# Attention weights of a four-layer graph network: the broadcast exponential moved from the scores to the weights, and due times taken from a backward play of the plan

## The chip, the cores and the metric

The kernel runs on one core of one Trainium2 chip, as one launch. A core has a matrix engine (TensorE, PE in the profile), a vector engine (VectorE, DVE), an engine for activation functions (ScalarE, ACT), a general one (GpSimd, POOL) and a queue engine that only issues transfers (SyncE, SP). Each works through its own instructions in the order in which the program gives them, and waits for the others by semaphores. The metric is the time of one execution on the device in microseconds (us).

## The reference

There are 64 graphs of 256 nodes with 256 features each (x, float32) and their adjacency matrices (adj, int32, about one entry in 64 is 1, the rest 0). Four layers follow each other, and each is added to x:

```python
h = relu(layernorm(x));  x = x + GAT0(h, adj)     # 4 heads of 64, slope 0.2, elu
h = relu(layernorm(x));  x = x + GAT1(h, adj)     # 4 heads of 64, slope 0.01, relu + residual, layer norm per head
h = relu(layernorm(x));  x = x + GAT2(h, adj)     # 1 head of 256, slope 0.2
h = relu(layernorm(x));  x = x + GRU(h, adj)      # 3 steps: aggregate adj^T (h w_i), then a GRU cell
```

An attention layer projects h to Wh, takes two scores of each node, `s` (as source) and `d` (as target), and weighs the neighbours by a softmax:

```python
e = leaky_relu(s[:, None] + d[None, :], slope)
alpha = softmax(where(adj > 0, e, -1e9), axis=-1)
out = alpha @ Wh
```

A GRU cell has six gate products of 256 by 256 per step: three from the aggregate and three from the state.

## The kernel before

**Tiling.** The 64 graphs are split into 33 units: one graph, 31 pairs of graphs, one graph. A unit goes through all four layers, and several units are in work at a time, so that one unit's matrix work fills the other's waits. Nodes lie on the 128 partitions; a pair has C = 4 chunks of 128 nodes.

**The weights.** exp(leaky_relu(s + d)) isn't computed as written. With a = slope, exp(max(t, a t)) for t = s + d is the larger of exp(s) exp(d) and exp(a s) exp(a d); a factor that depends only on the node whose softmax it is cancels, so that one needs only max(f0, f1 · cb): `f0` = exp(score) and `f1` = exp(a · score) of the node on the partition, and `cb` = exp((a − 1) · score of the target), the same on all partitions. The adjacency enters as a `cap`: where there is no edge the cap is tiny, and the minimum of weight and cap masks it.

`factors` makes these. The scores are columns of the projected tile `wh`. For the first SPREAD = 2 units TensorE spreads the target's scores over all partitions into a PSUM bank (`spread`, matmuls L1092), and ScalarE writes the exponential of it to `cb` (L1099). For the others TensorE transposes the score columns (L1111), ScalarE takes the exponential of the short `row` (L1118), a DMA on ScalarE's queue stores it to DRAM (`rd`, L1123), and a DMA on SP's queue loads it back to all partitions (L1124; 1024 KB for a pair with 4 heads, 256 KB with one). Two small ScalarE exponentials make f0 and f1 (L1130).

`weights` makes one head's tile `pt`. For each graph and each chunk of 128 nodes there is one VectorE TENSOR_SCALAR over 128 x 256 elements, cb times f1, then max with f0 (L1145); then one TENSOR_TENSOR over the whole head of a pair (128 x 1024) takes the minimum with `cap`. `attend` multiplies pt with wh (L1163).

**The order.** Nothing is issued as it is written. Every operation is recorded in `_Schedule` with its engine, a cost in ns and the buffers that it reads and writes; then `run` plays the program forward on modelled engines. At each free engine it takes the operation with the earliest due time that is ready and whose buffers have a free slot, and the resulting order is what each engine gets. Results are visible to another engine after OVERLAP + HOP (370, 240, 240 and 270 ns for PE, ACT, DVE and POOL); a DMA takes 2000 ns plus its bytes at 220 per ns. Due times come from one pass backwards over the operations: the due time of a follower less STRETCH (3.13) times its cost less MARGIN (800), counted from the end of the unit, which is set by PACE (104000 ns per pair). Operations with `port=True` (VectorE's and GpSimd's with shared access) aren't planned at the same time.

**Names in the profile.** `vec` records most VectorE and GpSimd operations and `op` some of ScalarE's, so many instructions carry L829. The layer norm is L997 (statistics on VectorE), L1006 and L1007 (GpSimd), L1015 (ScalarE, out `xn` or, ahead of the GRU, `hn`), its transposition L1032. The projection is L1054 (PE, with weights `w0e`, `w1e`, `w2e` by layer) and the copies L1067 and L1069. In the first 75 us PE also multiplies weight matrices (L949) and a few columns (L927). Layer 0 loads xt and the adjacency `at`, makes `am` (L1220), `cap_n` (L1214, L1230) and its transposition. Layer 1's norm per head is L1296 and L1297 (GpSimd, tile `mean`). The GRU splits the state in two parts (`hl`, L1346, `split`), aggregates (L1361, copied to `ag`), and multiplies the gates (L1375, in `bank`, with `ht` the transposed state); ScalarE's activations make `g` from `bank` and VectorE combines them; L1389 transposes states and outputs (`rows_of`), L1449 stores the output. Pools have a few slots: 8 PSUM banks, 5 `xt`, 4 `pt`, 2 `cb` for 4 heads.

Of the kernel before, what the change touches and what calls it, by code (L numbers as in the profile page):

```python
# [518 lines left out]
SPREAD = 2  # L519
PACE = 104000.0  # L520
# [8 lines left out]
class _Buf:  # L529


    def __init__(self, cls, shape, dtype, tile=None):
        self.cls, self.shape, self.dtype, self.tile = cls, shape, dtype, tile
        self.parts = {}
        self.left = 0
        self.slot = None


class _Op:
    __slots__ = (  # L540
        "engine", "cost", "port", "emit", "group", "bufs", "takes", "nbytes", "succs", "waits", "due", "ready",
        "index",
# [3 lines left out]
class _Schedule:  # L546
# [10 lines left out]

    OVERLAP = {"pe": 0, "act": 90, "dve": 80, "pool": 0, "sp": 0}
    HOP = {"pe": 370, "act": 240, "dve": 240, "pool": 270, "sp": 0}
# [3 lines left out]
    STRETCH = 3.13  # L563
    MARGIN = 800.0

    def __init__(self, tc, pools):

        self.tc, self.pools = tc, pools
        self.last = {}
        self.free = {cls: list(range(n)) for cls, (_, n) in pools.items()}  # L570
        self.ops = []
        self.group = 0
        self.end = {}
# [4 lines left out]
    def op(self, engine, cost, emit, reads=(), writes=(), takes=(), nbytes=0, port=False):  # L578
        o = _Op()
        o.port = port  # L580
        o.engine, o.cost, o.emit, o.group, o.nbytes = engine, cost, emit, self.group, nbytes
        o.succs, o.index, o.ready = [], len(self.ops), 0.0
        deps, o.bufs, o.takes = set(), [], []
        for written, items in ((False, reads), (True, writes)):
            for item in items:
                b, part = item if isinstance(item, tuple) else (item, None)
                if b not in o.bufs:
                    o.bufs.append(b)
                    b.left += 1
                if written and b.tile is None and b not in o.takes:  # L590
                    o.takes.append(b)
                keys = list(b.parts) if part is None else [k for k in (part, None) if k in b.parts]
                for k in keys:
                    writer, readers = b.parts[k]
                    if writer is not None:
                        deps.add(writer)
                    if written:
                        deps.update(readers)
# [7 lines left out]
        for b in takes:  # L606
            if b.tile is None and b not in o.takes:
                o.takes.append(b)
        deps.discard(o.index)
        o.waits = len(deps)  # L610
        for d in deps:
            self.ops[d].succs.append(o)
# [22 lines left out]
    def enable(self, ops, able):  # L635
        for o in ops:
            o.waits -= 1
            if o.waits == 0:
                heapq.heappush(able[o.engine], (o.due, o.index))

    def roomy(self, o):
        need = {}
        for b in o.takes:
            if b.tile is None:
                need[b.cls] = need.get(b.cls, 0) + 1
        return all(len(self.free[c]) >= n for c, n in need.items())

    def start(self, o, clock):
        for b in o.takes:
            if b.tile is None:  # L650
                b.slot = heapq.heappop(self.free[b.cls])
                b.tile = self.pools[b.cls][0].tile(b.shape, b.dtype, name=f"{b.cls}{b.slot}")
        self.issue(o)
        self.trace.append((clock, o))

    def run(self):
        ops = self.ops
        for o in reversed(ops):
            late = self.end[o.group]
            for s in o.succs:  # L660
                if s.group == o.group or o.group not in self.end or o.group < 0:
                    late = min(late, s.due - self.STRETCH * s.cost - self.MARGIN)
            if o.nbytes:
                late -= self.DMA_LATENCY + o.nbytes / self.DMA_RATE
            o.due = late
        engines = ("pe", "act", "dve", "pool", "sp")
        able = {e: [] for e in engines}
        idle = dict.fromkeys(engines, True)
        events = []
        clock = self.dma_free = self.port_free = 0.0  # L670
        count = 0
# [5 lines left out]

        for o in ops:
            if o.waits == 0:
                heapq.heappush(able[o.engine], (o.due, o.index))  # L680
        done = 0
        self.trace = []
        while True:
            for e in engines:
                if not idle[e]:
# [848 lines left out]
```

## Time and profile before

| what | us |
|---|---|
| three runs | 3197.56, 3197.72, 3199.27 (median 3197.72) |
| the profiled execution | 3199.95 |
| its span, first to last instruction | 3198.1 |
| GpSimd busy in the span | 897.4 |
| gate matmuls (L1375), share of the chain that ended last | 55% |
| granted TensorE clock, mean | 0.996 |

The span is what the trace covers; the execution's time has 1.85 us around it. The chain that ended last is found by going back from the last instruction, at each step to what released it:

```profile
PE 87%; DVE 9%; POOL 2%; ACT 1%; issue 1%; DMA 0%; SPq 0%; ACTq 0%; POOLq 0%; DVEq 0%
```

In 40 equal slices of 80 us, each digit the busy share in tenths, TensorE, VectorE and ScalarE look like this:

```profile
PE   7899999999999999999999999999999999999998
DVE  7777867778767778767678677788677787677753
ACT  5454444454454444454444454544444444544433
```

A row of the views by line gives the line, the engine, the operation, out<-in by the program's names, the shapes, the count, the busy time in us and the mean duration of one in ns, then the idle time of the engine just before these instructions and what ended it. In the timeline a row gives the start, the length, the engine, the line and the count, and in brackets the idle time before.

### The profile page before, as it was taken

Reading aid. Unit: us, or ns where it says so; the run is one execution under the profiler, and the core shown is the slowest. Engines: PE = TensorE matmul, PEld = TensorE weight load, DVE = VectorE, ACT = ScalarE, POOL = GpSimd, SP = SyncE. Lnnn points to the kernel's source line nnn. Section 1 sums busy time; section 2 is a strip of 40 time slices with the busy share of each in tenths; the row PEclk is TensorE's granted clock in tenths of the full one; section 3 lists DMA queues with packets and bytes.
Section 4 is the critical chain, followed back from the end, with each engine's and each line's share of the span. In section 5 each row is a group of like instructions: output and inputs, shape, how many; then the busy total and the mean of one; then the engine's idle time right before and its main releaser. Section 6 shows DMA issues by size and latency. Waiting matters only on the chain.

```text
span 3198.1 us, 48707 instructions
## 1 busy us (share of the span) xinstructions
PE 3143.2 (98%) x18599; PEld 1931.9 (60%) x18599; DVE 2321.4 (73%) x5206; ACT 1486.8 (46%) x3128; POOL 897.4 (28%) x907
## 2 busy tenths in 40 slices
PE   7899999999999999999999999999999999999998
PEld 6765656565666655566656566556566556665555
DVE  7777867778767778767678677788677787677753
ACT  5454444454454444454444454544444444544433
POOL 4323332133331233331233321333311333311210
PEclk9999999999999999999999999999999999999999
DMA  4110111101111101111101111111111011101000
GB/s 129 34 49 29 54 54 34 47 31 50 54 54 34 47 31 50 54 47 34 53 28 54 53 36 45 40 41 54 54 34 47 31 50 50 47 23 44 11 16 12
DMA packets 109927, 138.82 MB, mean 43 GB/s; under 512 B 44714, under 2 KB 97524, under 8 KB 102004
## 3 DMA queue, kind: packets, MB, share of 16 engines
q1 hardware_dynamic: 105712, 134.25, 12.8%
q8 instruction: 149, 2.44, 0.3%
q10 hardware_dynamic: 3972, 1.36, 0.2%
q14 instruction: 94, 0.77, 0.1%
HBM read 109.84 MB, written 17.34 MB: 40 GB/s over the span
## 4 chain that ended last, share of the span: by engine, by line
PE 87%; DVE 9%; POOL 2%; ACT 1%; issue 1%; DMA 0%; SPq 0%; ACTq 0%; POOLq 0%; DVEq 0%
PE bank L1375 55%; PE bank L1054 10%; PE bank L1163 10%; PE bank L1361 5%; PE bank L1032 3%; PE bank L1389 2%; DVE pt L1145 2%; DVE g L829 2%; DVE pt L829 1%; POOL mean L1297 1%; POOL o L829 1%; DVE o L829 1%; ACT ht L829 1%; DVE xt L1308 1%; DVE mean L829 1%
## 5 line engine op out<-in xcount | busy, mean ns | idle before, releaser
L1375 PE MATMUL bank<-ag,wc 128*128 128x512 f32 (+1 forms) x2376 | 1063.0, 582 | 0.0
L1375 PE MATMUL bank<-ht,whh 128*128 128x512 f32 (+1 forms) x2376 | 1055.6, 580 | 2.2 <-ACT g L829 1.3
L829 ACT ACTIVATE g<-bank,bg 128x512 f32<-128x512 f32 (+1 forms) x594 | 395.2, 670 | 713.6 <-PE bank L1375 706.6
L1375 PEld LDWEIGHTS bank<-ag,wc 128*128 128x128 f32 x2376 | 441.4, 190 | 459.2 <-issue 441.1
L1375 PEld LDWEIGHTS bank<-ht,whh 128*128 128x128 f32 x2376 | 435.0, 190 | 438.9 <-issue 424.2
L1006 POOL TENSOR_SCALAR mv<-mv 128x4 f32<-128x4 f32 (+1 forms) x132 | 81.9, 621 | 1428.6 <-DVE mv L998 1383.6
L1145 DVE TENSOR_SCALAR pt<-cb,f 128x256 f32<-128x256 f32 x1152 | 416.9, 430 | 6.0 <-ACT cb L1099 5.2
L1163 PEld LDWEIGHTS bank<-wh,pt 128*64 128x64 f32 (+1 forms) x8704 | 345.6, 142 | 94.4 <-issue 76.1
L829 DVE SCALAR_TENSOR_TENSOR g<-g,g 128x512 f32<-128x512 f32 (+1 forms) x396 | 263.3, 670 | 180.4 <-ACT g L829 180.4
L1163 PE MATMUL bank<-wh,pt 128*64 128x65 f32 (+1 forms) x8704 | 382.0, 233 | 9.7 <-DVE pt L829 5.8
L829 DVE TENSOR_TENSOR pt<-pt,cap 128x1024 f32<-128x1024 f32 (+1 forms) x297 | 341.3, 1193 | 0.1
L829 DVE SCALAR_TENSOR_TENSOR g<-bank,g 128x512 f32<-128x512 f32 (+1 forms) x198 | 129.8, 666 | 280.2 <-PE bank L1375 280.0
L829 DVE SCALAR_TENSOR_TENSOR g<-g,ht 128x512 f32<-128x512 f32 (+1 forms) x198 | 136.5, 689 | 172.0 <-ACT g L829 171.6
L1361 PE MATMUL bank<-am_r,hl 128*128 128x256 f32 x1536 | 238.1, 304 | 0.1
L1015 ACT ACTIVATE xn<-xt,mv 128x256 f32<-128x256 f32 x384 | 197.3, 588 | 72.1 <-DVE mv L829 71.9
L1361 PEld LDWEIGHTS bank<-am_r,hl 128*128 128x128 f32 x1536 | 198.2, 189 | 42.5 <-issue 30.6
L829 ACT COPY ag<-bank 128x512 f32<-128x512 f32 (+1 forms) x198 | 113.4, 573 | 233.4 <-PE bank L1361 230.1
L829 ACT ACTIVATE g<-g,bg 128x512 f32<-128x512 f32 (+1 forms) x198 | 137.6, 709 | 161.6 <-DVE g L829 159.4
L997 DVE BATCH_NORM_STATS2 st<-xt 128x6 f32<-128x256 f32 x512 | 208.1, 406 | 6.4 <-DMA xt<-in_x_dram 6.2
L829 ACT COPY ht<-bank 128x512 f32<-128x512 f32 (+1 forms) x264 | 137.8, 573 | 124.0 <-PE bank L1032 123.8
L1136 POOL MEMSET wh<- 128x16 f32 (+3 forms) x99 | 11.8, 120 | 635.5 <-ACT f L1130 635.5
L1007 POOL TENSOR_TENSOR mv<-mv,nhalf 128x4 f32<-128x4 f32 (+1 forms) x132 | 176.0, 1333 | 11.0
(91 smaller groups left out, 3452.2 us busy)
## 6 DMA issues: line engine op xcount, KB each, us to landing
cb<-rd SPq DMA_DIRECT2D x60, 1024.0 KB
xt<-in_x_dram SPq DMA_DIRECT2D x31, 512.0 KB
at<-in_adj_dram SPq DMA_DIRECT2D x31, 512.0 KB
out_dram<-xt SPq DMA_DIRECT2D x31, 512.0 KB
cb<-rd SPq DMA_DIRECT2D x30, 256.0 KB
cap<-cap_n SPq DMA_TRANSPOSE x128
cb<-rd SPq DMA_DIRECT2D x2, 512.0 KB
rd<-row ACTq DMA_DIRECT2D x60, 8.0 KB
```

What stands on the lines that cost most here:

```text
L829: emit = lambda: fn(*[a() if callable(a) else a for a in args], **kw)
L997: nc.vector.bn_stats(st.tile[:, c, :], xt.tile[:, c, :])
L1006: nc.gpsimd.tensor_scalar(mv.tile[:, 2, :], mv.tile[:, 1, :], 1e-5, None, op0=OP.add)
L1007: nc.gpsimd.tensor_tensor(mv.tile[:, 2, :], mv.tile[:, 2, :], nhalf[:, :C], op=OP.pow)
L1015: op("act", 610, lambda: nc.scalar.activation(xn.tile[:, c, :], xt.tile[:, c, :], AF.Relu, bias=mv.tile[:, 3, c : c + 1], scale=mv.tile[:, ...
L1032: nc.tensor.transpose(ps.tile[:, c * P : (c + 1) * P], xn.tile[:, c, dc * P : (dc + 1) * P], ident)
L1054: nc.tensor.matmul(ps.tile[:, : heads * W], lhsT=ht.tile[:, dc, c * P : (c + 1) * P], rhs=we[:, dc].rearrange("p h w -> p (h w)"), start=( ...
L1145: nc.vector.tensor_scalar(pt.tile[:, b, jc, :].rearrange("p (i n) -> p i n", n=P), cb.tile[:, h, 2 * b : 2 * b + 2, :], f.tile[:, 1, h, c ...
L1163: nc.tensor.matmul(ps[q * Q : (q + 1) * Q], lhsT=pt.tile[:, b, jc, i0 : i0 + Q], rhs=wh.tile[:, h, 2 * b + jc, :w], start=(jc == 0), stop= ...
L1361: nc.tensor.matmul(ps.tile[:, b * N : (b + 1) * N], lhsT=hl.tile[:, k, 2 * b + sc, :], rhs=am.tile[:, 2 * b + sc, :], start=(k == 0 and sc ...
L1375: nc.tensor.matmul(ps.tile[:, :S], lhsT=w[:, dc, g * P : (g + 1) * P], rhs=v.tile[:, dc, :], start=(first and dc == 0), stop=(last and dc ...
L1389: nc.tensor.transpose(ps.tile[:, c * P : (c + 1) * P], ht.tile[:, j, c * P : (c + 1) * P], ident)
```

## The change

It has three parts.

1. **The weights.** The target's score is broadcast as it is, without an exponential. ScalarE then computes exp((a − 1) · target's score + a column) for every graph, chunk and head (128 x 256), where the column is now the logarithm of the old f1, a · score plus a constant. One VectorE operation in place (SCALAR_TENSOR_TENSOR, 128 x 256) takes the max with f0 and the min with cap; the multiply-and-max and the wide minimum are gone. f1's small exponential becomes a small VectorE operation, the exponential of the row a copy.
2. **The first units.** SPREAD goes from 2 to 3. Units below it have no `cb`: ScalarE reads the scores of each head from the PSUM bank, which is held until all its weights are made.
3. **The planner.** `play` is the old forward play, without issuing anything. `latest` plays the program backwards from its end, taking operations by their start times of the last play, latest first, and gives each its latest start; these are the next play's due times. `run` makes up to 7 plays and issues the order of the one with the shortest modelled span. HOP becomes 310, 180, 180 and 210, PACE 100000, STRETCH 3.46. The part of `split` in the diff calls the same operations as before.

Counted over the program, VectorE loses 1152 TENSOR_SCALAR of 128 x 256, 279 TENSOR_TENSOR of 128 x 1024 and 18 of 128 x 512, and gets 1152 SCALAR_TENSOR_TENSOR of 128 x 256 and 99 small operations. ScalarE gets 1152 exponentials of 128 x 256, 90 of them from PSUM, and loses 18 copies of `cb` and 99 small exponentials. Three stores `rd` and three loads `cb` go; TensorE has 72 more matmuls in `spread` and 3 transposes fewer.

```diff
-SPREAD = 2
-PACE = 104000.0
+SPREAD = 3
+PACE = 100000.0
...
-    HOP = {"pe": 370, "act": 240, "dve": 240, "pool": 270, "sp": 0}
+    HOP = {"pe": 310, "act": 180, "dve": 180, "pool": 210, "sp": 0}
...
-    STRETCH = 3.13
+    STRETCH = 3.46
     MARGIN = 800.0
+    ROUNDS = 7
...
+    def lag(self, o, s):
+        if o.nbytes:
+            return self.DMA_LATENCY + o.nbytes / self.DMA_RATE
+        return 0 if o.engine == s.engine == "pe" else self.OVERLAP[o.engine] + self.HOP[o.engine]
...
+    def latest(self, starts):
+        left = {o.index: len(o.succs) for o in self.ops}
+        able = {e: [] for e in self.ENGINES}
...
+        def ready(o):
+            heapq.heappush(able[o.engine], (-starts[o.index], o.index))
...
+                o = self.ops[index]
+                if pred >= 0:
+                    left[pred] -= 1
+                    if left[pred] == 0:
+                        ready(self.ops[pred])
+                    continue
+                idle[o.engine] = True
+                for p in sorted(o.preds):
+                    heapq.heappush(events, (clock + self.lag(self.ops[p], o), count, p, index))
+        span = max(before_end.values())
+        return {i: span - t for i, t in before_end.items()}
...
+    def run(self):
+        due = self.paths()
+        self.span = float("inf")
+        for _ in range(self.ROUNDS):
+            trace, slots, span = self.play(due)
+            if span < self.span:
+                self.trace, taken, self.span = trace, slots, span
+            elif span == float("inf"):
+                break
+            due = self.latest({o.index: clock for clock, o in trace})
...
-                op("pe", pe(880), emit, [wh], [ps], takes=[cb])
-                op("act", act(700), lambda: nc.scalar.activation(
-                    cb.tile[:, h].rearrange("p c n -> p (c n)"), ps.tile[:, :S], AF.Exp,
-                    scale=slope - 1.0, bias=-shift * (slope - 1.0),
-                ), [ps], [(cb, h)])
+                op("pe", pe(880), emit, [wh], [ps])
+                return ps

             if u < SPREAD:
-                for h in range(heads):
-                    spread(h)
+                cb = [spread(h) for h in range(heads)]
...
-                    nc.scalar.activation(
-                        row.tile, ps.tile[:R, :P], AF.Exp, scale=slope - 1.0, bias=-shift * (slope - 1.0)
-                    )
+                    nc.scalar.copy(row.tile, ps.tile[:R, :P])
...
-            exps(0, 1.0)
-            exps(1, slope)
+            op("act", 225, lambda: nc.scalar.activation(
+                f.tile[:, 0], wh.tile[:, :, :, width], AF.Exp, bias=-shift
+            ), [wh], [(f, 0)])
+            vec(nc.vector.tensor_scalar, 180, lambda: f.tile[:, 1], lambda: wh.tile[:, :, :, width],
+                slope, (1 - 2 * slope) * shift, op0=OP.mult, op1=OP.add, reads=[wh], writes=[(f, 1)])
...
-        def weights(cap, f, cb, h):
+        def weights(cap, f, cb, h, slope):
             pt = buf("pt", [P, nb, 2, N])
...
-                nc.vector.tensor_scalar(
-                    pt.tile[:, b, jc, :].rearrange("p (i n) -> p i n", n=P),
-                    cb.tile[:, h, 2 * b : 2 * b + 2, :],
-                    f.tile[:, 1, h, c : c + 1], f.tile[:, 0, h, c : c + 1], op0=OP.mult, op1=OP.max,
-                )
+                op("act", 475, lambda: nc.scalar.activation(
+                    pt.tile[:, b, jc, :], source(h, b), AF.Exp,
+                    scale=slope - 1.0, bias=f.tile[:, 1, h, c : c + 1],
+                ), [cb[h] if u < SPREAD else (cb, h), (f, 1)], part)
+                vec(nc.vector.scalar_tensor_tensor, 426, lambda: pt.tile[:, b, jc, :],
+                    lambda: pt.tile[:, b, jc, :], lambda: f.tile[:, 0, h, c : c + 1],
+                    lambda: cap.tile[:, b, jc, :], op0=OP.max, op1=OP.min,
+                    reads=[cap, (f, 0)], writes=part, port=True)
...
-                    op("dve", 425, lambda b=b, jc=jc: emit(b, jc), [(cb, h), f], [(pt, (b, jc))], port=True)
-            vec(nc.vector.tensor_tensor, dve(1240), lambda: pt.tile, lambda: pt.tile, lambda: cap.tile, op=OP.min,
-                reads=[cap], writes=[pt], port=True)
+                    direct(b, jc)
             return pt
```

## The prediction

> **What bounds the kernel now.** I read the busy shares first, then the windows of the start, of one period of the steady state and of the end, then TensorE's waits, then its timeline around those, and last the durations by shape.
>
> ```profile
> PE 3143.2 (98%) x18599; PEld 1931.9 (60%) x18599; DVE 2321.4 (73%) x5206; ACT 1486.8 (46%) x3128; POOL 897.4 (28%) x907
> ```
>
> TensorE (PE) is busy 98% of the span of 3198.1 us, so 54.9 us are all that any other engine can give back without less PE work. The windows show where these lie (columns: length, then busy time of PE, weight loads, VectorE, ScalarE, GpSimd, granted clock):
>
> ```profile
> 0.00:50.00 50.00, 32.51 (x290) 25.89 (x292) 34.16 (x111) 28.12 (x80) 19.61 (x41) 0.97 0.56 160
> 50.00:100.00 50.00, 40.32 (x509) 35.75 (x506) 44.51 (x123) 22.75 (x66) 18.60 (x22) 0.93 0.14 48
> 100.00:150.00 50.00, 44.88 (x215) 37.58 (x214) 33.91 (x89) 28.73 (x71) 19.05 (x26) 0.94 0.18 54
> 150.00:203.30 53.30, 53.30 (x445) 37.85 (x445) 49.66 (x114) 24.97 (x57) 21.94 (x21) 1.00 0.10 36
> 979.43:1076.34 96.91, 96.73 (x572) 58.45 (x572) 71.84 (x160) 45.74 (x95) 28.05 (x27) 1.00 0.13 45
> 3130.00:3198.10 68.10, 55.09 (x226) 40.08 (x225) 21.63 (x48) 20.55 (x42) 0.00 (x0) 0.93 0.04 13
> ```
>
> The start leaves PE idle for 17.5 + 9.7 + 5.1 = 32.3 us, and from 150 us on it is full. In the steady state one pair of graphs takes 96.91 us, of which PE works 96.73; VectorE has 25 us to spare there, ScalarE 51. The end, from 2918.5 us, has 17.8 us of idle in its five windows, 7.6 of them after the last matmul (3190.45 to 3198.1), which are the last store. TensorE's waits by what released them (total, times, longest), first from 0 to 203.3 us, then from 203.3 to 2918.5, then to the end:
>
> ```profile
> PE bank L1032 <- ACT xn L1015: 16.5, 6, 9.9
> PE bank L1163 <- DVE pt L829: 5.8, 1, 5.8
> PE bank L1163 <- POOL mean L1296: 3.7, 1, 3.7
> ```
> ```profile
> PE bank L1389 <- ACT ht L829: 2.9, 17, 0.2
> ```
> ```profile
> PE bank L1389 <- DVE ht L829: 7.2, 6, 1.8
> ```
>
> In 28 periods the largest wait adds up to 2.9 us: the middle is worth nothing to a faster VectorE. The start is a chain of layers of the first graphs, in which VectorE's attention weights (pt) hold PE for 5.8 us at one place and the layer norms behind them hold it at others. PE is slower after such a wait:
>
> ```profile
> 78.97 3.95 PE L1163 MATMUL bank<-wh,pt 128*64 128x65 f32 x128
> 88.78 3.74 PE L1163 MATMUL bank<-wh,pt 128*64 128x65 f32 x64 [5.85 <-DVE pt L829]
> 92.73 2.09 PE L1163 MATMUL bank<-wh,pt 128*64 128x65 f32 x64 [0.22 <-DVE o L829]
> ```
>
> The same 64 matmuls take 3.74 us after the gap and 2.09 four microseconds later. Likewise 8 matmuls take 3.66 after the 3.7 us wait at 106 us (1.90 normally) and 3.73 at 14 us; the excess at the start sums to some 7 us. At 3174 us 8 matmuls take 3.44 after only 1.85 us idle (normally 1.89).
>
> [...]
>
> **The change part by part.** The durations (count | busy, mean ns):
>
> ```profile
> L1145 DVE TENSOR_SCALAR pt<-cb,f 128x256 f32<-128x256 f32 x1152 | 416.9, 430 | 6.0 <-ACT cb L1099 5.2 <-DMA cb<-rd 0.7
> L829 DVE TENSOR_TENSOR pt<-pt,cap 128x1024 f32<-128x1024 f32 x279 | 326.1, 1213 | 0.0
> L829 DVE SCALAR_TENSOR_TENSOR ht<-g,g 128x256 f32<-128x256 f32 x12 | 4.7, 418 | 0.1
> L829 DVE SCALAR_TENSOR_TENSOR xt<-bank,rs,xt 128x256 f32<-128x256 f32 x128 | 57.8, 473 | 1.1
> L829 ACT ACTIVATE g<-bank,bg 128x256 f32<-128x256 f32 x36 | 17.0, 472 | 14.7 <-PE bank L1375 14.1 <-DVE rs L829 0.5
> L829 ACT ACTIVATE g<-g,bg 128x256 f32<-128x256 f32 x12 | 6.1, 506 | 11.7 <-DVE g L829 11.7
> L1015 ACT ACTIVATE xn<-xt,mv 128x256 f32<-128x256 f32 x384 | 197.3, 588 | 72.1 <-DVE mv L829 71.9
> ```
>
> *VectorE, steady state.* A pair has 9 heads (4 + 4 + 1). Removed: 36 multiply-and-max of 0.430 and 9 wide minima of 1.213, 26.4 us. Added: 36 fused max-and-min of 0.418 to 0.473 (bounds: the plain one, and the dearest with a scalar pointer), 15.0 to 17.0 us, and 3 small column operations at 0.163 (the row of 128x4), 0.5. So 71.8 becomes 60.9 to 62.9.
>
> [...]
>
> *ScalarE, steady state.* Added: 36 exponentials with a column as bias. The trace has none of just this kind; the rows around it are 0.472 (from PSUM), 0.506 (SBUF, bias column) and 0.588 (SBUF, bias and scale columns). I take 0.506, whose operands are the same: 18.2 us (17.0 to 21.2), less 0.7 for three small ones. So 45.7 becomes 63.2 (62.0 to 66.2) of 96.9. ScalarE has room; whether it has it at the right moment is a rival below. The row's exponential becomes a copy on the same engine, priced at nothing: its 0.26 us are covered by ScalarE's idle third.
>
> *PE.* With SPREAD 3 the third unit's scores are spread by 72 more matmuls in place of three transposes: 32 such took 3.67 us, so 72 × 0.1147 − 3 × 0.11 = +7.9 us, 5.5 of it (48) ahead of the first GRU step. Three round trips of scores (row store, broadcast load) leave the ScalarE and SP queues; they ran beside full engines, and I give them nothing.
>
> *The start.* The order comparison shows the same kinds of PE work ahead of the first GRU matmul (116.99 us), plus the 48. VectorE has 66 multiply-and-max, 12 wide and 9 half-wide minima ahead of it in the old order. Consecutive ones overlap; from start to start they take 0.322, 1.137 and 0.68, in all 66 × 0.322 + 12 × 1.137 + 9 × 0.68 = 41.0 us. In the new order 66 fused ones at 0.345 (0.425 less the overlap of 0.08) and 6 small ones take 23.4: 17.6 us less on the engine that was busy 44.5 of 50 us there. ScalarE gets 66 × 0.38 = 25 us more and loses about 10. It was busy 22.8 of the 50, so it stays below VectorE's old load. Of the 32.3 us idle, 12.8 come before any weight is made (first norm 9.9, weights' preparation 2.96), and 3.1 wait for the next unit's norm; 16.4 can go. I take 13 (0 to 16), since the layer norms' chain itself stays. Fewer long gaps return 3 of the 7 us of slow clock (0 to 5). With PE's own +7.9 the start gives −8.1.
>
> *The planner.* In the middle it can only lose. Before, PE lost 4.7 us in 28 periods. The new plan allows 60 ns less per hand-over; three GRU steps per pair hand over twice each, so if the chip needs what the old plan allowed, 28 × 6 × 0.06 = 10 us are lost. I take 2 (0 to 9), near the old total, because PE's filler at these places in the new order, 10 to 12 matmuls of 0.429, exceeds the chain of 3.3 to 4.2 us (tanh 0.69, four VectorE operations of 0.6 to 0.7, hand-overs). What the earlier outputs now wait for is covered likewise: a store is done 2.7 us after issue, the next load 2.5 later, against about 16 us of filler before that tile is needed. In the end the new order sets work of the last pairs between the last graph's steps: of 10.2 us idle before the last matmul I take 5 (0 to 10). 1 us of slow clock (0 to 1.6) goes with it. The tail may grow by 1 (0 to 1.5), since a 512 KB store now stands directly ahead of the last 256 KB in SP's queue.
>
> *Sum.* −13 − 3 + 7.9 + 2 − 5 − 1 + 1 = −11.1; span 3198.1 − 11.1 = 3187.0. The profiled execution took 3199.95, 1.85 above its span; the median of the runs is 3197.72, 2.23 below that. So 3187.0 + 1.85 − 2.23 = 3186.6, say 3187. All bounds good: −24.7, 3173; all bad: +18.4, 3216.
>
> **The rivals.** (A) *The start gives back what it gains.* The chain in front of the first GRU step is then PE's extra rows and the layer norms; 8 us gained, 7.9 paid, the end unchanged: 3198. For it: only 5.8 us of the start's waits name the weights. Against: the norms wait behind the same VectorE work.
>
> (B) *Slower: exponentials stand in ScalarE's queue ahead of the gates.* In-order, up to sixteen stand in a row in the new order, in front of five gate activations, two aggregate copies (ag), and through these the next gate matmuls. The plan gives each 0.385 us of the engine (475 less 90). At 0.506 less the same overlap, 0.416, a stretch is 0.5 us late; at 0.588 less 0.094, 0.494, it is 1.7 late, as much as one bank's four matmuls (4 × 0.429) cover. From there it decides: each further 0.05 us of duration costs 16 × 0.05 = 0.8 us per pair, 28 × 0.8 = 22 us: 3187 + 22 = 3209. Against: the nearest row is 0.506.
>
> (C) *A larger gain.* Start and end lose all that can go: 16 + 5 − 7.9 + 11.6 = 24.7: 3173. Against: each is an end of its bound.
>
> (D) *The held scores starve the start.* The first three units now keep their scores in PSUM banks, of 8, until all heads' weights are made; earlier a 0.6 us copy freed them. If PE waits one head's four exponentials and four fused operations (some 3 us) twice per layer and unit beyond what is saved, 3 × 2 × 3 = 18 us are lost: 3187 + 18 = 3205. For it: 2 to 4 banks per layer are held. Against: the planner counts the banks.
>
> **How the numbers follow.** Forecast 0.55; A 0.17; B 0.12; C 0.10; D 0.06. A run of this kernel can tell 0.2% (6.4 us) from no change: faster is below 3191.3, slower above 3204.1. The forecast's own range is 3178 to 3196, of which about nine tenths are faster; with C that makes 0.60. A, the rest of the forecast and half of D lie within 0.2%: 0.25. B and half of D are slower: 0.15. The range of 8 in 10 cuts C's far end and B's far half: 3171 to 3206.
>
> **What would show it.** PE busy near 3143 + 4 to 8 and a period of 96.9 to 97.2 us in the middle; ScalarE near 63 and VectorE near 62 us per period; no 5.8 us wait for pt at the start; the first gate matmul at 104 to 112 us rather than 117; idle in 0 to 203 us of 17 to 20 us; the exponential's row at 0.47 to 0.51 us. It is wrong if PE waits for ag or ht in the middle by more than 10 us in all (B), if the start's idle stays above 28 (A, D, the latter with waits on free banks), or if the period grows although PE doesn't wait.

## The result, and the profile after

The changed kernel takes 3279.51 us (median of four runs, 3278.54 to 3281.47) against 3198.14: a ratio of 1.0255, 95% interval 1.0243 to 1.0267. It is slower by 81 us where 11 us less were forecast, and far outside the range. The profiled execution took 3280.0 us, its span is 3278.1.

Line numbers are later in the changed kernel: L900 is the recording helper (L829 before), L1215 the new exponential, L1447 the gate matmuls, L1433 the aggregation, L1461 the transposes of states and outputs; the runs with the planner of before keep the old numbers, and the one with passes cut in four has L1450 for the gates. The first part of the page and the windows of the start, the middle and the end (length, then busy time of PE, weight loads, VectorE, ScalarE, GpSimd, granted clock):

```profile
PE 3167.2 (97%) x18668; PEld 1946.7 (59%) x18668; DVE 2179.5 (66%) x5008; ACT 1907.8 (58%) x4160; POOL 798.2 (24%) x907
```
```profile
0.00:203.30 203.30, 184.13 (x1565) 148.19 (x1566) 151.02 (x428) 142.05 (x368) 81.59 (x114) 1.00 0.23 67
203.30:3000.00 2796.70, 2715.75 (x15897) 1634.91 (x15896) 1885.93 (x4274) 1642.04 (x3542) 681.12 (x749) 0.99 0.14 42
3000.00:3278.10 278.10, 267.36 (x1208) 163.62 (x1206) 142.53 (x308) 123.72 (x251) 35.49 (x44) 0.99 0.06 20
```

VectorE's busy time fell and no engine is near its limit but TensorE. TensorE's idle time before and after: 32.3 and 19.2 at the start, 4.8 and 81.0 in the middle (from 203.3 us to 2918.5 before, to 3000 after), 17.9 and 10.7 at the end. That is −13.1 + 76.2 − 7.2 = +56; with 24 us more of TensorE's own busy time it makes the 80 us of the span. Start and end gained as forecast. The middle lost 76 us of waiting, in these places (waited for, total, times, longest):

```profile
PE bank L1447 <- DVE g L900: 32.4, 14, 3.2
PE bank L1447 <- ACT g L900: 29.3, 26, 1.7
PE bank L1433 <- DVE o L900: 7.9, 12, 0.7
PE bank L1461 <- DVE xt L900: 7.7, 25, 0.3
```

The middle is some 14 periods of two pairs, and the same few waits come again in nearly each of them, once or twice. Two such periods:

```profile
766.17:968.06 201.89, 195.98 (x1143) 117.99 (x1143) 135.13 (x307) 118.59 (x257) 48.65 (x54) 0.99 0.14 43
968.06:1168.31 200.25, 194.34 (x1143) 117.35 (x1143) 135.12 (x307) 118.59 (x257) 48.57 (x54) 1.00 0.14 43
```

Two pairs took 193.8 us before and take 200 to 202 now, of which 5.9 are waits. VectorE needs 67.6 us per pair and ScalarE 59.3, both far below the period, so it is no lack of throughput. What happens is seen in the timeline around one of the 13 waits of 2.3 us or more for VectorE's g (start, length, engine, line, in brackets the idle time before), ScalarE first, then VectorE, then GpSimd, then TensorE:

```profile
1044.94 6.48 ACT L1215 ACTIVATE pt<-cb,f 128x256 f32<-128x256 f32 x16
...
1045.67 2.85 DVE L900 SCALAR_TENSOR_TENSOR pt<-pt,f,cap 128x256 f32<-128x256 f32 x7
1048.44 0.68 DVE L900 TENSOR_TENSOR o<-o,mean 128x512 f32<-128x512 f32 x1
1049.04 2.70 DVE L900 SCALAR_TENSOR_TENSOR pt<-pt,f,cap 128x256 f32<-128x256 f32 x4
1051.66 0.68 DVE L900 TENSOR_TENSOR o<-o,mean 128x512 f32<-128x512 f32 x1
1052.27 5.09 DVE L900 SCALAR_TENSOR_TENSOR pt<-pt,f,cap 128x256 f32<-128x256 f32 x5
1057.28 1.28 DVE L900 SCALAR_TENSOR_TENSOR g<-g,g 128x512 f32<-128x512 f32 x2
1058.49 0.68 DVE L900 SCALAR_TENSOR_TENSOR g<-bank,g 128x512 f32<-128x512 f32 x1
...
1049.20 1.46 POOL L900 TENSOR_TENSOR o<-o,gamma_b 128x512 f32<-128x512 f32 x1
1052.42 1.45 POOL L900 TENSOR_TENSOR o<-o,gamma_b 128x512 f32<-128x512 f32 x1 [1.75 <-DVE o L900]
1053.83 2.85 POOL L900 TENSOR_TENSOR o<-o,beta_b 128x512 f32<-128x512 f32 x2
...
1059.22 1.98 PE L1447 MATMUL bank<-ht,whh 128*128 128x512 f32 x4 [2.32 <-DVE g L900]
```

Sixteen fused operations stand ahead of the gates' operations (g) in VectorE's queue. The first seven take 2.85 us together. The next four include one and the last five include three that start while GpSimd is in a pass of layer 1's norm (gamma, beta): five take 5.09 us instead of 2.06 (4 × 0.396 + 0.48). Behind them `g<-g,g` and `g<-bank,g`, which reads a PSUM bank and so frees it, come late, and TensorE waits 2.32 us for that bank. In another period the granted clock is 0.50 behind the same wait (857.21 to 860.62 us; at 1059 us it is 1.00):

```profile
857.33 3.60 PE L1447 MATMUL bank<-ht,whh 128*128 128x512 f32 x4 [2.33 <-DVE g L900]
```

These four matmuls take 3.60 us, 1.62 more than at 1059 us. Behind eight of the 13 waits the granted clock is 0.50 and the four take 3.33 to 3.78 us; behind the other five it is 1.00 and they take 1.98 or 1.99. In the stretches of the middle at 0.50 TensorE is busy for 29.3 us; by estimate, if that work takes half the time at 1.00, they cost 14.6 us. Beside the 7.9 of the added spreading that is most of TensorE's 24 us; smaller terms of both signs were not worked out (the first matmul behind a wait takes 0.70 us, not 0.59, and the start's granted clock is 1.00, where it was 0.93 to 0.97 in the first 150 us). The two new kinds of operation over the whole program, and the shortest, median and longest fused operation in ns:

```profile
L900 DVE SCALAR_TENSOR_TENSOR pt<-pt,f,cap 128x256 f32<-128x256 f32 x1152 | 556.6, 543 | 56.9 <-ACT pt L1215 55.6
L1215 ACT ACTIVATE pt<-cb,f 128x256 f32<-128x256 f32 x1062 | 443.3, 497 | 4.6 <-DVE rs L900 3.4 <-PE bank L1234 0.7 <-ACT pt L1215 0.3
...
L900 DVE SCALAR_TENSOR_TENSOR pt<-pt,f,cap x1152: 453/480/1529, 20.7 to 3174.3; 128x256 f32<-128x256 f32 x192
```

The exponential is as forecast. The fused operation's mean is 0.543; its median is 0.480 and its longest 1.529. Seventy-five took over 0.83 us ("held" from here on), 73 us above the median in all. All 75 start while a GpSimd instruction runs, 71 of them in a gamma, beta or bias pass; and every fused operation that starts in such a pass is held.

### The profile page after: what moved, and what is told of

Same layout as the page of the kernel before. It is cut to its first block, busy times and chain, and to the rows that moved or that the text cites. A ratio compares the mean times of both kernels' runs of the same rounds, so it can differ in the third digit from the quotient of the medians.

```text
span 3278.1 us, 49825 instructions
## 1 busy us (share of the span) xinstructions
PE 3167.2 (97%) x18668; PEld 1946.7 (59%) x18668; DVE 2179.5 (66%) x5008; ACT 1907.8 (58%) x4160; POOL 798.2 (24%) x907
## 4 chain that ended last, share of the span: by engine, by line
PE 63%; DVE 29%; POOL 3%; issue 2%; ACT 2%; DMA 0%; ACTq 0%; POOLq 0%; SPq 0%; DVEq 0%
PE bank L1447 44%; DVE pt L900 13%; PE bank L1125 7%; PE bank L1234 4%; DVE g L900 4%; DVE o L900 4%; PE bank L1103 3%; PE bank L1433 2%; POOL o L900 2%; PE bank L1461 2%; DVE st L1068 2%; DVE mean L900 2%; ACT g L900 1%; DVE xt L900 1%; DVE ht L900 1%
## 5 line engine op out<-in xcount | busy, mean ns | idle before, releaser
L1447 PE MATMUL bank<-ht,whh 128*128 128x512 f32 (+1 forms) x2376 | 1076.6, 588 | 48.7 <-DVE g L900 32.4
L1447 PE MATMUL bank<-ag,wc 128*128 128x512 f32 (+1 forms) x2376 | 1047.3, 582 | 17.0 <-ACT g L900 14.4
L1447 PEld LDWEIGHTS bank<-ag,wc 128*128 128x128 f32 x2376 | 445.6, 191 | 531.7 <-issue 493.9
L1447 PEld LDWEIGHTS bank<-ht,whh 128*128 128x128 f32 x2376 | 439.0, 192 | 493.5 <-issue 388.7
L900 DVE SCALAR_TENSOR_TENSOR pt<-pt,f,cap 128x256 f32<-128x256 f32 x1152 | 556.6, 543 | 56.9 <-ACT pt L1215 55.6
L900 ACT ACTIVATE g<-bank,bg 128x512 f32<-128x512 f32 (+1 forms) x594 | 393.1, 670 | 273.6 <-PE bank L1447 238.7
L900 ACT ACTIVATE g<-g,bg 128x512 f32<-128x512 f32 (+1 forms) x198 | 140.2, 708 | 538.2 <-DVE g L900 538.0
L1215 ACT ACTIVATE pt<-cb,f 128x256 f32<-128x256 f32 x1062 | 443.3, 497 | 4.6 <-DVE rs L900 3.4
L1077 POOL TENSOR_SCALAR mv<-mv 128x4 f32<-128x4 f32 (+1 forms) x132 | 44.6, 338 | 1501.5 <-DVE mv L1069 1347.8
L900 DVE SCALAR_TENSOR_TENSOR g<-g,g 128x512 f32<-128x512 f32 (+1 forms) x396 | 275.8, 699 | 187.0 <-ACT g L900 186.9
L900 DVE SCALAR_TENSOR_TENSOR g<-bank,g 128x512 f32<-128x512 f32 (+1 forms) x198 | 132.7, 670 | 272.4 <-PE bank L1447 270.9
L1086 ACT ACTIVATE xn<-xt,mv 128x256 f32<-128x256 f32 x384 | 205.1, 595 | 65.6 <-DVE mv L900 65.6
L1433 PE MATMUL bank<-am_r,hl 128*128 128x256 f32 x1536 | 234.3, 304 | 9.1 <-DVE o L900 7.9
L1433 PEld LDWEIGHTS bank<-am_r,hl 128*128 128x128 f32 x1536 | 195.6, 189 | 57.6 <-issue 47.2
L900 DVE SCALAR_TENSOR_TENSOR g<-g,ht 128x512 f32<-128x512 f32 (+1 forms) x198 | 133.2, 673 | 141.3 <-ACT g L900 141.1
L900 DVE TENSOR_SCALAR f<-wh 128x16 f32<-128x16 f32 (+3 forms) x99 | 45.9, 463 | 188.2 <-ACT wh L1140 185.7
L900 ACT COPY ag<-bank 128x512 f32<-128x512 f32 (+1 forms) x198 | 111.1, 570 | 83.6 <-PE bank L1433 82.9
L1140 ACT COPY wh<-bank 128x258 f32<-128x258 f32 (+1 forms) x256 | 93.0, 377 | 105.8 <-PE bank L1125 104.4
L900 ACT COPY ht<-bank 128x512 f32<-128x512 f32 (+1 forms) x264 | 140.5, 577 | 21.5 <-PE bank L1103 21.3
```

The source lines that it names most:

```text
L900: emit = lambda: fn(*[a() if callable(a) else a for a in args], **kw)
L1077: nc.gpsimd.tensor_scalar(mv.tile[:, 2, :], mv.tile[:, 1, :], 1e-5, None, op0=OP.add)
L1086: op("act", 610, lambda: nc.scalar.activation(xn.tile[:, c, :], xt.tile[:, c, :], AF.Relu, bias=mv.tile[:, 3, c : c + 1], scale=mv.tile[:, ...
L1140: nc.scalar.copy(wh.tile[:, :, c, :], src)
L1215: op("act", 475, lambda: nc.scalar.activation(pt.tile[:, b, jc, :], source(h, b), AF.Exp, scale=slope - 1.0, bias=f.tile[:, 1, h, c : c + ...
L1433: nc.tensor.matmul(ps.tile[:, b * N : (b + 1) * N], lhsT=hl.tile[:, k, 2 * b + sc, :], rhs=am.tile[:, 2 * b + sc, :], start=(k == 0 and sc ...
```

## The experiments

Three theories stood at the start. (1) The plan gives a fused operation 0.346 us of VectorE, the chip takes more, and the order has no slack for it where blocks of them stand ahead of gates. (2) The new planner's order breaks by its thin hand-overs and latest due times, whatever the weights. (3) The new weights cost this much in any order. The first four runs cross weights and planner and change one number of the plan each.

**New weights, planner of before** (SPREAD 3, with PACE, STRETCH, HOP and the single play of before):

```diff
 # kernel before, plus:
-SPREAD = 2
+SPREAD = 3
 # and factors, weights of the changed kernel
```

> The new weights and SPREAD 3, with the planner, PACE, STRETCH and HOP of before. Theory 1 (the plan gives a fused VectorE operation 0.346 us of the engine, the chip takes 0.396 and more, and blocks of them stand ahead of the gates' VectorE work): the same cost is planned here, but with the wider hand-overs of before; 3210 to 3260. Theory 2 (the new planner's thin hand-overs and latest due times make an order that breaks, whatever the weights): no loss, 3185 to 3200. Theory 3 (the new weights cost this in any order): about 3280.

Measured: 3183.2 us (ratio 0.9953, 0.993 to 0.9975).

```profile
203.30:2918.50 2715.20, 2714.28 (x16049) 1647.36 (x16048) 1881.59 (x4303) 1651.63 (x3581) 690.24 (x752) 1.00 0.13 44
```
```profile
PE bank L1389 <- DVE ht L829: 0.9, 1, 0.9
```

In the middle TensorE now waits 0.9 us in all. Theory 3 falls: the weights gain 15 us. Theory 1 in its plain form (3210 to 3260) missed too, since the same 426 ns is planned here and nothing is lost; only 4 fused operations are held.

**Weights of before, new planner** (SPREAD 2):

```diff
 # changed kernel, with factors and weights of before, plus:
-SPREAD = 3
+SPREAD = 2
```

> The weights and SPREAD of before, with the new planner and its constants. Theory 1: the plan's costs fit, so 3180 to 3200. Theory 2: the loss is here, 3250 to 3280. Theory 3: 3180 to 3200.

Measured: 3202.49 us (1.0011, 1.0 to 1.0023). The largest wait in the middle:

```profile
PE bank L1447 <- ACT g L900: 15.5, 27, 2.5
```

Theory 2 in its plain form falls: the new planner alone doesn't lose 80 us, but it gains nothing either. The loss needs both parts.

**The fused operation planned at 560 ns:**

```diff
-                vec(nc.vector.scalar_tensor_tensor, 426, lambda: pt.tile[:, b, jc, :],
+                vec(nc.vector.scalar_tensor_tensor, 560, lambda: pt.tile[:, b, jc, :],
```

> The changed kernel, but the plan counts a fused VectorE operation at 560 ns instead of 426 (its mean on the chip was 543). Theory 1: most of the loss goes, 3195 to 3220, and TensorE's waits in the middle fall from 81 us to under 25. Theory 2: the hand-overs are as thin as before, 3250 to 3280. Theory 3: 3270 to 3290.

Measured: 3184.91 us (0.9953, 0.9933 to 0.9972).

```profile
203.30:2918.50 2715.20, 2706.12 (x15980) 1639.02 (x15979) 1916.50 (x4284) 1639.52 (x3562) 675.50 (x749) 1.00 0.14 44
```

TensorE is idle there for 9.1 us. One number of the plan takes the whole loss away, more of it than theory 1 said (3195 to 3220). The number gives another order as well, so this run alone doesn't show that the cost as such is the cause.

**HOP of before in the changed kernel:**

```diff
-    HOP = {"pe": 310, "act": 180, "dve": 180, "pool": 210, "sp": 0}
+    HOP = {"pe": 370, "act": 240, "dve": 240, "pool": 270, "sp": 0}
```

> The changed kernel with the HOP of before (370, 240, 240, 270), the fused operation still planned at 426 ns. Theory 1: part of the loss goes, since wider hand-overs leave slack that late VectorE work can use, 3230 to 3270. Theory 2: most of the loss goes, 3195 to 3215. Theory 3: 3270 to 3290.

Measured: 3213.36 us (1.0046, 1.0026 to 1.0066), better than theory 1 said and at the edge of theory 2. In this order only 18 fused operations are held; whether the wider hand-overs help by their slack or by the fewer holds is not shown.

Next came direct trials on the changed kernel's own order, every engine's instructions in the same places.

**A shorter VectorE operation in the same order.** The mask of the adjacency is left out of the weights:

```diff
-                vec(nc.vector.scalar_tensor_tensor, 426, lambda: pt.tile[:, b, jc, :],
+                vec(nc.vector.tensor_scalar, 426, lambda: pt.tile[:, b, jc, :],
                     lambda: pt.tile[:, b, jc, :], lambda: f.tile[:, 0, h, c : c + 1],
-                    lambda: cap.tile[:, b, jc, :], op0=OP.max, op1=OP.min,
+                    3.0e38, op0=OP.max, op1=OP.min,
```

> The changed kernel in exactly its order; only the fused VectorE operation is replaced by a multiply-free one with a single tile as source (max with the column, min with a constant), so the mask of the adjacency is left out of the weights. Its kind took 0.322 us from start to start in the kernel before, less than the 0.346 planned. Theory 1 (the fused operation is longer than planned and the order has no slack for it): 3190 to 3225, TensorE's waits in the middle under 30 us. Rival (the order of the new planner waits in any case, by its thin hand-overs): 3255 to 3285.

Measured: 3177.79 us (0.9937, 0.9914 to 0.9959).

```profile
L900 DVE TENSOR_SCALAR pt<-pt,f x1152: 321/348/1393, 20.3 to 3071.2; 128x256 f32<-128x256 f32 x192
```
```profile
PE bank L1447 <- DVE g L900: 12.9, 14, 1.8
```

The columns of the first line are shortest, median and longest in ns. The order that took 3279 takes 3178 when this operation is 0.13 us shorter, so the order itself doesn't force the loss. Yet 62 of them are still held (more than 0.35 us above the median, 1.393 at most): holds with shorter operations between them don't make the loss.

**Shorter GpSimd passes in the same order:**

```diff
-                vec(nc.gpsimd.tensor_tensor, pool(1290), lambda: o.tile[:, hs], lambda: o.tile[:, hs],
-                    lambda: each(gamma_b), op=OP.mult, reads=[B_gamma], writes=part, engine="pool", port=True)
+                vec(nc.gpsimd.tensor_tensor, pool(1290), lambda: o.tile[:, hs, :, :8], lambda: o.tile[:, hs, :, :8],
+                    lambda: each(gamma_b)[:, :, :, :8], op=OP.mult, reads=[B_gamma], writes=part, engine="pool", port=True)
 # and the same for bias_b and beta_b
```

> The changed kernel in exactly its order; only GpSimd's three passes of layer 1's norm per head (bias, gamma, beta) cover 8 of the 64 columns of each head, the rest is left out (it adds zeros and multiplies by one with these inputs). In the changed kernel 75 of the 1152 fused operations took over 0.83 us, 75 us above the median in all, beside such a pass. If these collisions carry the loss: under 25 of them, 3180 to 3225. If the fused operation's plain length (0.396 against 0.346 planned, 1.8 us per pair) carries it: 3250 to 3280.

Measured: 3176.1 us (0.9929, 0.9908 to 0.9951), 3 fused operations held.

```profile
L900 DVE SCALAR_TENSOR_TENSOR pt<-pt,f,cap 128x256 f32<-128x256 f32 x1152 | 488.9, 483 | 58.2 <-ACT pt L1215 56.2 <-DMA cap<-cap_n 0.8
...
L900 POOL TENSOR_TENSOR o<-o,gamma_b 128x64 f32<-128x64 f32 x62 | 34.6, 560 | 78.1 <-DVE o L900 78.1
```
```profile
1021.08 2.25 DVE L900 SCALAR_TENSOR_TENSOR pt<-pt,f,cap 128x256 f32<-128x256 f32 x5
```
```profile
PE bank L1461 <- DVE xt L900: 8.6, 26, 0.9
```

The five fused operations that took 5.09 us take 2.25, and no wait for VectorE's or ScalarE's g is left in the middle; the largest that is left is the one for `xt`. The passes' own chain is shorter here as well, so the run doesn't wholly separate the holds from that chain. But the holds are gone for all of VectorE's work: in the changed kernel 179 of its operations lasted over 0.35 us beyond the median of their kind, 177 us in all; here 11 did, 7 us in all.

**Passes cut in four, all work done, same order:**

```diff
+                def quarters(t, what):
+                    for q in range(0, E, E // 4):
+                        view = o.tile[:, hs, :, q : q + E // 4]
+                        nc.gpsimd.tensor_tensor(view, view, each(t)[:, :, :, q : q + E // 4], op=what)
...
-                vec(nc.gpsimd.tensor_tensor, pool(1290), lambda: o.tile[:, hs], lambda: o.tile[:, hs],
-                    lambda: each(gamma_b), op=OP.mult, reads=[B_gamma], writes=part, engine="pool", port=True)
+                op("pool", pool(1290), lambda: quarters(gamma_b, OP.mult), [B_gamma], part, port=True)
 # and the same for bias_b and beta_b
```

> The changed kernel in exactly its order and with all its work; each of GpSimd's passes for bias, gamma and beta is issued as four instructions over a quarter of the columns. If a fused operation is held until the GpSimd instruction beside it ends, it is held for at most a quarter as long each time, but may be held more often: 3185 to 3240. If GpSimd takes its share by its busy time, however it is cut: 3270 to 3300, since the quarters are busy at least as long as the whole.

Measured: 3257.53 us (1.0185, 1.0168 to 1.0202), between the two. Holds are shorter but more frequent: 155 fused operations start in a quarter pass, none of them takes over 0.693 us, and the operations are 33 us above their median in all, where it was 73. (The 3 over 0.83 us stand beside other GpSimd work at the start.) The five take 2.87 us. But a pass is now four instructions of 0.614, longer in sum than one of 1.5. The waits for VectorE's g fall from 32.4 to 6.9 us; those for ScalarE's g stay (29.3 before), and waits for `ag` come up:

```profile
L1354 POOL TENSOR_TENSOR o<-o,gamma_b 128x128 f32<-128x128 f32 x248 | 144.9, 614 | 48.0 <-DVE o L900 48.0
```
```profile
PE bank L1450 <- ACT g L900: 34.6, 26, 1.6
PE bank L1450 <- ACT ag L900: 14.0, 13, 1.3
...
PE bank L1450 <- DVE g L900: 6.9, 13, 1.1
```

So the holds got shorter with the GpSimd instruction (at most 0.693 beside 0.614), but cutting it is no remedy. That the passes' longer sum makes the waits that are left is likely, and not shown.

**The planned cost again, at 480 and 520 ns:**

```diff
-                vec(nc.vector.scalar_tensor_tensor, 426, lambda: pt.tile[:, b, jc, :],
+                vec(nc.vector.scalar_tensor_tensor, 480, lambda: pt.tile[:, b, jc, :],
 # and 520
```

> The changed kernel with the fused operation planned at 480 ns, 0.400 us of the engine, which is the chip's start to start without contention (0.396), but not its mean duration. Theory 1: most of the loss goes, 3190 to 3225. Rival (chance: which order a planned cost gives): anywhere from 3185 to 3290.

> The changed kernel with the fused operation planned at 520 ns, 0.440 of the engine, near the mean on the chip less the overlap (0.463). Theory 1 (planned VectorE time decides, 480 falls short of the mean): 3185 to 3215. Rival (which order comes out is chance, 560 a lucky one): anywhere from 3185 to 3290.

Measured: 3286.66 (1.0276, 1.0246 to 1.0306) and 3247.02 (1.0151, 1.0129 to 1.0173), both against theory 1's numbers and both within what the rival, chance, allows. A cost below 426 was not measured. At 480 the same stretch stands in the new order, VectorE then TensorE:

```profile
1058.27 5.08 DVE L900 SCALAR_TENSOR_TENSOR pt<-pt,f,cap 128x256 f32<-128x256 f32 x5
```
```profile
1065.21 3.78 PE L1447 MATMUL bank<-ht,whh 128*128 128x512 f32 x4 [4.91 <-DVE g L900]
```

Five fused operations in 5.08 us again, and a wait of 4.91 behind them. Planning the plain length (480 less the plan's overlap of 80 is 0.400; the chip shows 0.396 from start to start) doesn't cover the holds.

**The thin HOP with the planner of before** (new weights, SPREAD 3):

```diff
 # new weights, planner of before, plus:
-    HOP = {"pe": 370, "act": 240, "dve": 240, "pool": 270, "sp": 0}
+    HOP = {"pe": 310, "act": 180, "dve": 180, "pool": 210, "sp": 0}
```

> The new weights with the planner of before (one play, due times from the paths, PACE and STRETCH of before), the fused operation at 426, but with the thin HOP of the change. If thin hand-overs are what makes the wrong cost hurt: 3225 to 3280. If it takes due times from the backward play: 3178 to 3200, as with the wide ones (3183).

Measured: 3185.3 us (0.996, 0.9944 to 0.9976); one fused operation held. Thin hand-overs alone aren't the cause.

**One play only, with the new constants:**

```diff
-    ROUNDS = 7
+    ROUNDS = 1
```

> The changed kernel with one play only: due times from the paths as before, but with the new STRETCH, PACE and HOP. If the backward play's due times are what puts the fused operations beside GpSimd's passes: under 15 fused operations over 0.83 us, and a time near or below this plan's own span of 3241, 3200 to 3240. If the new constants do it: 30 or more, and a time above its plan, 3250 to 3320.

Measured: 3296.59 us (1.0306, 1.0286 to 1.0327); 34 held. The backward play isn't needed for the loss: due times from the paths under PACE 100000 and STRETCH 3.46 put fused operations beside the passes too. It differs from the run before only in PACE and STRETCH and the order that these give; which of the two does it was not tried. Its own plan is 56 us longer than that of the changed kernel, so a part of its time was planned.

**Two variants of the good one.** SPREAD 2 with the new weights and the planner of before, and 560 ns there:

```diff
-SPREAD = 3
+SPREAD = 2
 # and, in the other, 426 -> 560
```

> The new weights with the planner of before, as in the run of 3183, but SPREAD 2: 7.9 us less of TensorE, and the third unit's weights wait for the round trip of its scores. If the third unit's spreading pays: 3184 to 3192. If it costs only TensorE's time: 3174 to 3179.

> The new weights with the planner of before and SPREAD 3, the fused operation planned at 560 ns. If the planner of before already leaves slack enough for the longer operation: 3180 to 3188, no change against 3183. If the wrong cost was paid there too: 3170 to 3178.

Measured: 3175.81 us (0.9929, 0.9912 to 0.9947) and 3185.99 (0.9961, 0.9946 to 0.9976). SPREAD 3 costs 7.4 us where the weights are fast, about what TensorE's added matmuls were reckoned to take (7.9). The wrong cost isn't paid for in that order. The first is the best of all that compute everything, ahead of both kernels of the case; from 203.3 to 3000 us TensorE is idle for 0.1:

```profile
203.30:3000.00 2796.70, 2796.60 (x16510) 1696.76 (x16509) 1932.22 (x4410) 1696.80 (x3675) 711.36 (x770) 1.00 0.13 43
```

**The runs against their plans.** The schedule ends each plan with a span of its own. Beside it the measured span of the profiled execution, and the held weight operations (fused ones over 0.83 us; where the kind differs, the weights' operation of 128x256 that stands in its place, more than 0.35 above its median):

| kernel | plan's span | measured span | difference | held |
|---|---|---|---|---|
| before | 3217.5 | 3198.1 | −19 | 30 |
| new weights, planner of before, SPREAD 2 | 3196.1 | 3173.4 | −23 | 2 |
| same, SPREAD 3 | 3200.8 | 3182.9 | −18 | 4 |
| same, 560 | 3199.1 | 3183.0 | −16 | 3 |
| same, thin HOP | 3191.5 | 3183.5 | −8 | 1 |
| weights of before, new planner | 3186.7 | 3200.6 | +14 | 33 |
| changed | 3185.0 | 3278.1 | +93 | 75 |
| changed, fused planned at 480 | 3205.7 | 3286.5 | +81 | 49 |
| changed, 520 | 3188.4 | 3244.7 | +56 | 52 |
| changed, 560 | 3202.3 | 3185.5 | −17 | 51 |
| changed, HOP of before | 3203.3 | 3211.5 | +8 | 18 |
| changed, one play | 3241.4 | 3295.0 | +54 | 34 |
| changed, passes in four | 3185.0 | 3255.7 | +71 | 3 |
| changed, shorter operation | 3185.0 | 3175.6 | −9 | 62 |
| changed, shorter passes | 3185.0 | 3174.3 | −11 | 3 |

In the eight rows without a loss the chip is 8 to 23 us faster than the plan. With the fused operation under-planned, the excess over the plan falls as its planned cost rises, 93, 81, 56, −17, though the holds hardly change from 480 to 560. So a hold need not hurt. It doesn't follow that the larger cost gave VectorE room: from the first hold to the next `g<-bank,g` the plans at 426, 480, 520 and 560 leave VectorE 1.8, 0.1, 0.2 and 0.0 us idle. At 560 the sixteen operations, three of them held, run in one piece of 10.36 us where 7.68 were planned:

```profile
1033.12 10.36 DVE L900 SCALAR_TENSOR_TENSOR pt<-pt,f,cap 128x256 f32<-128x256 f32 x16
...
1043.99 1.28 DVE L900 SCALAR_TENSOR_TENSOR g<-bank,g 128x512 f32<-128x512 f32 x2
```

But TensorE has other matmuls meanwhile: it is busy for 17.08 of the 17.10 us from 1029.58 on. Here a hold hurt where TensorE needed the bank soon behind it (the wait of 2.32 us in the changed kernel). That a larger planned cost brings such an order about, rather than the chance of which order comes out, these four plans don't show. In the changed kernel's own order, a shorter operation or shorter passes each suffice.

The plan's own times for the stretch shown at the top say how it adds up. From its first fused operation to the first gate operation behind it, VectorE falls 4.8 us further behind the plan: four holds of 1.05 each, and 0.05 for each of the twelve others (0.396 against 0.346). The plan had left 1.8 us of room ahead of `g<-bank,g`, which is therefore 3.0 us late; 2.32 of that comes out as TensorE's wait.

## Why the prediction was wrong

*The step that failed* is the sentence "In the middle it can only lose": it took 2 us with bounds of 0 to 9, counted from hand-overs alone (28 × 6 × 0.06, which gives 10, above its own bound). The middle lost 76 us of waiting and, by the estimate above, 14.6 at a granted clock of 0.50. The bound had no term for VectorE: it was held to have room because its sum per pair was about 62 us of 97, although that sum says nothing of the 11.6 us from 1045.67 in which sixteen fused operations and two others stand ahead of a gate's three operations. The covering argument, 10 to 12 matmuls of filler against a chain of 3.3 to 4.2 us, counted the chain without its queue.

*The fused operation's size*, 0.418 to 0.473, came from means of 12 and 128 operations of other kinds. It measured 0.480 in the median, and 0.543 with the holds. The 0.430 of the operation that it replaced was a mean with holds in it, too; in the medians 0.480 came for 0.406. The trace of before had the sign of the holds:

```profile
L1145 DVE TENSOR_SCALAR pt<-cb,f x1152: 392/406/1425, 19.4 to 3107.7; 128x256 f32<-128x256 f32 x192
```

The multiply-and-max reached 1.425 us, and 29 of its 30 held ones stood beside a gamma, beta or bias pass. Only its mean was used. This case's five fused operations in 5.09 us beside the passes, and in 2.25 with the passes short, tie the holds to the passes; the form with one tile as source is held too, up to 1.393. By what mechanism, no run here shows.

*Rival B* had the right shape: a long row of weight work in an in-order queue ahead of the gates, with the loss coming back each period. It stood on the wrong engine. Sixteen exponentials take 6.48 us, 0.405 each, between the planned 0.385 and the 0.416 reckoned. What follows them on ScalarE is late: the wait of 1.09 us at 1053.19 stands directly behind them. But with the passes short all 29.3 us of waits for ScalarE's g are gone at the same exponentials. Rivals A and D are answered by the start, which gained as forecast and names no wait for free banks of scores.

*The change of due times* was priced as if the new order were as robust as the old. The planner exempts VectorE and GpSimd from overlapping by planning them one after the other; the order on each queue alone did not make the chip do so here. In the stretch shown, the first gamma pass was planned 1.2 us behind the last of the sixteen operations and began during the eighth, as soon as its input was ready.

*What held.* The start: 19.2 us idle (17 to 20 said), no 5.8 us wait for weights. The end: 7.2 us less idle (5 less, and 1 more of tail). The exponential 0.497 (0.506). TensorE's added matmuls: 7.4 us between the two SPREAD runs (7.9).

*What was off without deciding.* The first gate matmul came at 100.79, earlier than 104 to 112, and the start's granted clock is 1.00 where it was 0.93 to 0.97, so by estimate more than the 3 us forecast came back. ScalarE needs 59.3 us per pair (62 to 66): the sum added up whole durations, but in a row the exponentials start every 0.40 us. VectorE needs 67.6 (60.9 to 62.9). There, too, durations were added up: counting overlaps once, the multiply-and-max took 416.9 / 1152 = 0.362 each, so that 13.0 us per pair went and not 15.5, and the fused operation took 556.6 / 1152 = 0.483, so that 17.4 came and not 15.0 to 17.0. The rest of the 5 to 7 us stays open.

In the planner of before, the new weights with SPREAD 3 gave 3183.2. The forecast without its planner's terms (2 − 5 − 1 + 1) is 3190, 7 us from that; the rest of the error is the planner's term, with the weights in its order.

## What to carry to other kernels

A planner's order is worth what its costs are worth: after a new operation is put in, compare its plan with the trace in that very order, holds included, and don't read an engine's room from its sum per period but from the queue ahead of the operation that frees the bottleneck's buffer. Where the plan keeps two engines apart only on paper, expect them to meet, as 71 fused operations and GpSimd's passes did here. When a change bundles a cheaper operation with a tighter schedule, run each half alone: here the new weights alone gained 15 us (22 with SPREAD 2), the new planner alone lost 4, and the two together lost 81.

## What the runs showed of the hardware

- A fused VectorE operation of 128x256 that starts beside a GpSimd pass of 128x512 takes up to 1.53 us in the changed kernel instead of 0.48; in the median it ends 0.28 us after the pass. All 71 that started in such a pass were held. With the passes cut in four the longest beside a quarter is 0.69, at 0.614 us per quarter.
- In the middle of the changed kernel twelve waits of 2.32 to 2.34 us stand ahead of the same four gate matmuls. Behind seven of them the granted clock was 0.50 for most of the four, which took 3.33 to 3.62 us; behind five it was 1.00 and they took 1.98 or 1.99. Behind the thirteenth wait, of 3.19 us, they took 3.78 at 0.50. Why the clock fell in some periods and not in others is not shown.
- A VectorE max-and-min of 128x256 with one tile, a column and a constant takes 0.348 us in the median (0.263 from start to start), less than the multiply-and-max with one tile and two columns before (0.406, 0.323) and the two-tile one (0.480, 0.396).
